# Neighbour quantiles in a four-layer graph kernel: gathers that skip pad columns, products over all partitions, and other set-up and ends

## The chip, the cores and the metric

One core of one Trainium2 chip runs the whole kernel, in one launch. The metric is device time in microseconds: the median of three runs of the kernel before is 2677.36 us. The engines are named as in the profile: PE (TensorE), PEld (PE's loading of the stationary operand), DVE (VectorE), ACT (ScalarE), POOL (GpSimd), SP (SyncE, which issues the DMAs).

## The reference

There are 32 graphs of 512 nodes with 64 channels each, in float32, and for each graph a dense 512x512 matrix of edge weights, of which about 1.6% plus the diagonal are not zero. Four layers follow one another, each as `x = layernorm(x + layer(x))`.

```python
# layer 0: A / max(deg, 1) @ x
# layer 1: Chebyshev polynomials of the normalized Laplacian, 4 orders, weights, bias
# layer 2: logmap in the hyperbolic ball for all pairs, sigmoid of an attention logit, * adj, sum
# layer 3:
adj_d = _dilate_adj(adj, mask)            # with more than 10 neighbours: each (m+1)//2-th is removed, both ways
vals = where(adj_d > 0, x[:, None], big)  # per node: the values of its neighbours (and its own), per channel
sv = sort(vals, axis=2)
m = (adj_d > 0).sum(-1)
agg = 0
for tau, wt in zip([0.25, 0.5, 0.75], [0.25, 0.5, 0.25]):
    pos = tau * (m - 1)                   # linear interpolation between the two ranks around pos
    agg += wt * (sv[floor(pos)] * (1 - frac) + sv[ceil(pos)] * frac)
h = relu((x + agg) @ W1 + b1)             # 64 -> 128
y = (h @ W2 + b2) * mask                  # 128 -> 64
...
x = layernorm(x + y)
```

The change lies around layer 3: the sort of the neighbours' values per node and channel.

## The kernel before

**Order of the work.** All 32 graphs are written out as one list of operations. A class `Order` records each operation (`seq.op`), with its engine, an estimated duration and what it reads and writes. It then orders the list by itself: each operation belongs to a lane, and each lane has a due time from a table `STAGES` (L1341, in periods of 80 us per graph, from the first operation of the lane to the last); among ready operations the earliest due goes first. For PE a penalty (`STAY`) speaks against going over to a matmul of another array shape. Every engine then gets its instructions in that fixed order. So a change in one lane moves instructions of all others. Where PE would stand idle for long, the order puts in filler matmuls (`stay_active`, L1376), which write nowhere that is read.

**Lanes.** `front` loads a graph (four 128x512 tiles of the matrix and `XA` on SP's queue), transposes the matrix on PE into `front_AT`, copied by ACT (L469), and does layers 0 and 1. `pairs` and `tail` do layer 2. The reciprocal roots of the layernorms run on POOL (L694). `graph` makes the neighbour masks, the removal, and ranks the nodes by number of neighbours: `rk` holds the position of each node in that ranking, `perm` permutes by it, `slot` numbers the neighbours of each node. `gather`, `sort` and `head` do the quantiles; `finish` and `dense` bring them back to the nodes' own order and do the small network, the last layernorm and the store.

**Strips.** With the nodes ranked by neighbour count, slot s is needed by ever fewer nodes. Nodes stand in pairs, so that 256 columns hold 512 nodes: rows 0 to 63 have the channels of one half, rows 64 to 127 those of the other. The columns are cut in two strips. `HEAD` has the first 32 columns with 24 slots and is sorted for two graphs at once, in the array `SH`; `BODY` has the rest with 11 slots, in `SB`, one graph at a time:

```python
HEAD = Strip(0, [32] * 16 + [8] * 8, 2, ...)            # first column, widths of the slots, graphs
BODY = Strip(CUT, [224] * 8 + [132, 92, 52], 1, ...)
```

A table `UP` gives for each slot how many nodes have it at most, `LO` how many at least. The widths of some slots go beyond `UP`, because the sorting network works on equal widths: those columns are pads for every graph. (An operation at the end tests the tables against the data; outside them a slower path would run.)

**gather** (L1118). For each of seven groups of columns DVE makes a one-hot matrix `gather_oh` by comparing `slot` with a constant (L449, and L445 for the small slots); PE multiplies the node values, split into three bf16 parts (`tail_x3h`), with it into a `gather_bank` in PSUM, in 24 products of 128x64 shape. Then pad products (stationary `tabs[PADS]`, moving `ohm[PADS]`, both on rows 0 to 63) add 16384 wherever a node lacks the slot's neighbour, for the columns from `LO` to the width. ACT copies the bank into `SB` and `SH`.

**sort** (L1204) runs the network of minima and maxima on DVE (L445) within `SB`. Then rank products on PE (`tabs[RANKS]` with `ohm[RANKS]`, on rows 64 to 127) give the weight of each rank for each node; DVE multiplies (`sort_prod`), PE sums by transposing into the bank `PA`, ACT copies it to `sort_ap`. The column spans of these products are rounded[...] (`spans`, L1182). **head** (L1229) does the same for two graphs, with `PRS` in place of `sort_prod`, and then calls `finish` for one graph after the other.

**finish** (L1255) transposes `rk` (128x128 float32, with `identf`) on PE to spread positions along columns, makes four masks in two steps on ACT (`head_PT`), multiplies `sort_ap` with them, adds x and calls `dense`, with its buffers `oT`, `hT`, `zo`, one of each.

**Set-up** (L505 to L668) runs once before the ordered list: constants, identity matrices, the tables `tabs` (with two DVE copies per half), the weights (small loads on SP's queue, ahead of the first graph's matrix), and memsets of `tabs`, `SB`, `SH`, `PRS` on POOL (L1368 to L1371).

Of the kernel before, what the change touches and what calls it, by code (L numbers as in the profile page):

```python
# [85 lines left out]
class Strip:  # L86
# [3 lines left out]
    def __init__(self, first, W, G, order, low):  # L90
        self.first, self.W, self.G, self.order, self.low, self.K = first, W, G, order, low, len(W)
        self.off, self.tot = {}, 0
        for s in order:
            self.off[s] = self.tot
            self.tot += W[s] * G
        self.live = [(max(lo - first, 0), min(hi - first, W[s])) for s, (lo, hi) in enumerate(needed()[:self.K])]
        self.live = [x if x[0] < x[1] else (0, 0) for x in self.live]
        self.plans = [self.plan(0), self.plan(1)]
# [71 lines left out]
    {}))  # L170
BODY = Strip(CUT, [224] * 8 + [132, 92, 52], 1, [0, 2, 1, 3, 4, 6, 5, 7, 8, 9, 10], (
    {1: (0, 1, 2, 3), 2: (0, 1), 5: (0, 1), 7: (1,), 8: (2, 3)},
    {0: (4,), 1: (1, 3), 2: (2,), 3: (0, 1, 2), 4: (0, 1), 5: (2,), 6: (1, 2), 7: (1,), 8: (3,), 9: (0, 3)}))
# [229 lines left out]
def tile_adj_resnorm(ctx: ExitStack, tc: tile.TileContext, x, adj, nodemask, w1k, b1k, att_w, att_b,  # L403
# [16 lines left out]
    pools = {}  # L420

# [79 lines left out]
    def bank(dtype=F32):  # L501
        return seq.tile(pools["ps"], [P, 512 if dtype == F32 else 1024], dtype, "bank", bufs=BANKS.get(seq.lane, 2))


# [6 lines left out]
    identh = const.tile([P, P], BF16, name="identh")  # L511
    nc.vector.tensor_copy(identh, identf)
# [12 lines left out]
    with tc.tile_pool(name="first", bufs=1) as first:  # L525
        ii = first.tile([P, N], I32, name="ii")
        nc.gpsimd.iota(ii, pattern=[[1, 2], [2, H2]], base=0, channel_multiplier=0)
        nc.vector.tensor_copy(iotap, ii)
# [21 lines left out]
    nc.vector.tensor_copy(kf, ks)  # L550
    tb = const.tile([P, K], F32, name="tb")
    ts(tb, kf, part, PAD, op0=OP.is_ge, op1=OP.mult)

    tabs = const.tile([P, K, P], F16, name="tabs")
    nc.gpsimd.memset(tabs, 0.0)
    for h in range(2):
        nc.vector.tensor_copy(tabs[h * HM:(h + 1) * HM, :, h * D:(h + 1) * D],
                              tb[h * HM:(h + 1) * HM].unsqueeze(2).to_broadcast([HM, K, D]))
    PADS, RANKS = slice(0, 2 * HM), slice(2 * HM, P)
    acc = const.tile([P, K], F32, name="acc")  # L560
    nc.vector.memset(acc, 0.0)
    tn = const.tile([P, K], F32, name="tn")
    tau = const.tile([P, 1], F32, name="tau")
    for q, w in TAUS:
        ts(tau, part, -1.0, q, op0=OP.add, op1=OP.mult)
        ts(tau, tau, 0.0, None, op0=OP.max)
        ts(tb, kf, tau, None, op0=OP.subtract)
        ts(tn, tb, -1.0, None, op0=OP.mult)
        tt(tb, tb, tn, op=OP.max)
        ts(tb, tb, -1.0, 1.0, op0=OP.mult, op1=OP.add)  # L570
        ts(tb, tb, 0.0, w, op0=OP.max, op1=OP.mult)
        tt(acc, acc, tb, op=OP.add)
    for h in range(2):
        nc.vector.tensor_copy(tabs[(h + 2) * HM:(h + 3) * HM, :, h * D:(h + 1) * D],
                              acc[(h + 2) * HM:(h + 3) * HM].unsqueeze(2).to_broadcast([HM, K, D]))
# [13 lines left out]
    nc.sync.dma_start(wk[:, :, :D], w1k.rearrange("k u c o -> (k u c) o").rearrange("(g p) o -> p g o", p=P))  # L589
    def rows(src, n, name, m):  # L590
        t = const.tile([m, n], F32, name=name)
        nc.sync.dma_start(t, bass.AP(tensor=src.tensor, offset=src.offset, ap=[[0, m], [1, n]]))
        return t

    def parts3(src, name):

        rem, n = src, src.shape[-1]
        full = const.tile([3, n], F32, name=name + "s")
        part3 = const.tile([3, n], BF16, name=name + "p")
# [12 lines left out]
    b1f = const.tile([3, D + 2], F32, name="b1f")  # L612
    nc.sync.dma_start(b1f[:, :D], bass.AP(tensor=b1k.tensor, offset=b1k.offset, ap=[[0, 3], [1, D]]))
    attb = rows(att_b, 1, "attb", P)
    bias2 = parts3(rows(b2, D, "b2f", 3), "bias2")
    meanf = const.tile([D, D], F32, name="meanf")
    nc.vector.memset(meanf, 1.0 / D)
    attw = const.tile([D, 2], F32, name="attw")
    for k in range(2):
        nc.sync.dma_start(attw[:, k:k + 1], bass.AP(tensor=att_w.tensor, offset=att_w.offset + (1 - k) * D, ap=[[1, D], [1, 1]]))  # L620
    b1c = const.tile([D, 1], F32, name="b1c")
    nc.sync.dma_start(b1c, bass.AP(tensor=b1k.tensor, offset=b1k.offset, ap=[[1, D], [1, 1]]))

    wt = const.tile([P, D], F32, name="wt")
# [8 lines left out]
    for h in range(2):  # L633
        nc.sync.dma_start(w1s[h * D:(h + 1) * D], w1)
    b1s = const.tile([HID, 1], F32, name="b1s")
    nc.sync.dma_start(b1s, b1.rearrange("(h u) -> h u", u=1))
    w2s = const.tile([HID, D], F32, name="w2s")
    nc.sync.dma_start(w2s, w2)

    nmask = const.tile([P, T, B], F32, name="nmask")  # L640
    with tc.tile_pool(name="ps_0", bufs=1, space=PSUM) as ps, tc.tile_pool(name="masks", bufs=1) as masks:
        nm8 = masks.tile([B, N], U8, name="nm8")
        nc.sync.dma_start(nm8, nodemask)
        nmf = masks.tile([B, N], F32, name="nmf")
# [10 lines left out]
        wkT = const.tile([D, P], F32, name="wkT")  # L655
# [146 lines left out]
    def order(b, res):  # L802
# [14 lines left out]
        rk = seq.tile(pools["keep"], [P, T], F32, "rk", 8)  # L817
        ts(rk, sg, -0.5, 0.5 * N - 1.0, op0=OP.mult, op1=OP.add)
        perm = seq.tile(gm, [P, T, N], F16, "perm", 1, "nbT")
# [17 lines left out]
        if b % 2 == 0:  # L837
            res["ohm"] = seq.tile(pools["keep"], [P, 2, H2], F16, "ohm", 3)
# [4 lines left out]
        act(res["ohm"][:, b % 2, :], dist, AF.Relu, bias=1.0, scale=-1.0)  # L843
        res["slots"] = slot, rk
# [273 lines left out]
    def gather(b, res):  # L1118
# [3 lines left out]
        ohm = res["ohm"]  # L1122
        sl = slot.rearrange("p j (h n) -> p j h n", h=2)
        for g in GROUPS:
            pieces, at, x = [], {}, 0
            for piece in g:
                oh = seq.tile(pools["oh"], [P, T, 2, 448], F16, "oh", 2)
                w = 0
                for k, s in piece:
                    n, c = k.W[s], k.first  # L1130
# [18 lines left out]
            for i, ((k, s), o) in enumerate(at.items()):  # L1149
                n, lo = k.W[s], max(0, LO[s] // 2 - k.first)  # L1150
                if i == len(at) - 1:
                    lo = min(lo, n - 1)
                if lo < n:
                    assert o >= pieces[-1][1]
                    mm(pt[:, o + lo:o + n], tabs[PADS, s, :], ohm[PADS, b % 2, k.first + lo:k.first + n], start=False,
                       stop=(i == len(at) - 1))

            runs = []
            for (k, s), o in at.items():
                if runs and runs[-1][0] is k and runs[-1][3] == k.off[s]:  # L1160
                    runs[-1][2] += k.W[s]
                    runs[-1][3] += k.W[s] * k.G
                else:
                    runs.append([k, o, k.W[s], k.off[s] + k.W[s] * k.G, k.off[s]])
# [18 lines left out]
    for r, (lo, hi) in enumerate(BODY.live):  # L1183
        if hi > lo:
            lo = lo - lo % 32 if lo % P > 96 else lo - lo % 64 if lo % P >= 64 else lo - lo % P
# [18 lines left out]
    def sort(b, res):  # L1204
# [6 lines left out]
        for k, rs in enumerate(RB):  # L1211
            pt = bank()
            for r, lo, hi, o in rs:
                mm(pt[:, o:o + hi - lo], tabs[RANKS, r, :], ohm[RANKS, b % 2, CUT + lo:CUT + hi], start=True, stop=True)
# [14 lines left out]
    def head(b, res):  # L1229
# [4 lines left out]
        for k, rs in enumerate(RH):  # L1234
            pt = bank()
            n = (2 * CUT, CUT)[k]
            for i, (r, _, w) in enumerate(rs):
                mm(pt[:, n * i:n * i + 2 * w].rearrange("p (c g) -> p c g", g=2), tabs[RANKS, r, :],
                   ohm[RANKS, :, :w].rearrange("p g c -> p c g"), start=True, stop=True)
# [12 lines left out]
        for g in range(2):  # L1252
            finish(b - 1 + g, res["ends"][g], ap[:, g])

    def finish(b, end, ap):  # L1255
        rk, x3 = end
        pt = bank()
        for t in range(T):
            tr(pt[:, t * P:(t + 1) * P], rk[:, t:t + 1].to_broadcast([P, P]), identf)
# [15 lines left out]
    def dense(po, x3T, x3, dst, nm):  # L1275

        fin = pools["fin"]
        oT = seq.tile(fin, [P, N], F32, "oT", 1)
# [5 lines left out]
        ph = bank()  # L1284
        mm(ph[:HID, :], w1s, oT, start=True, stop=True)
        hT = seq.tile(fin, [HID, N], F32, "hT", 1)
        act(hT, ph[:HID, :], AF.Relu, bias=b1s)
        py = bank()[:, :T * D].rearrange("p (t n) -> p t n", n=D)
# [3 lines left out]
        z = wide("zo")  # L1292
# [330 lines left out]
```

## Time and profile before

| | |
|---|---|
| median of 3 runs | 2677.36 us (2675.84 to 2685.98) |
| the profiled execution | 2680.23 us, its span 2678.4 us |
| granted TensorE clock | 0.98 |
| busy PE, DVE | 2514.1 us, 2493.2 us |
| busy ACT, POOL | 1854.6 us, 352.9 us |
| DMA | 49.96 MB, mean 19 GB/s |
| instructions | 55594 |

The span is the traced part of one execution, from its first to its last instruction. Busy times are sums over an engine's instructions; register, branch, semaphore and DMA-issuing instructions are not in them. Rows of groups read: line, engine, operation, output, inputs, partitions x elements and type, count; then busy time, mean ns of one, and the idle time just before with what ended most of it. Rows of waits read: who waits, for whom, total us, times, mean us. In a timeline a row is a start, a duration and an instruction (or several alike), with the idle time before it and what ended it in brackets.

### The profile page before, as it was taken

How to read it: one execution, taken by the hardware profiler on the slowest of the kernel's cores; microseconds unless marked ns; L12 is line 12 of the kernel's file. 1: busy time of each engine (PE TensorE's matmuls, PEld its weight loads, DVE VectorE, ACT ScalarE, POOL GpSimd, SP SyncE). 2: the span in 40 equal slices, each digit the busy share in tenths (PEclk: the TensorE clock that was granted, in tenths of full speed). 3: DMA queues.
4: the chain of work that ended last, by engine and by line, in shares of the span. 5: the costliest groups of instructions: out<-in, count | busy, mean ns of one | idle time of the engine just before them, and what ended most of it. 6: DMA issues, size and time to landing. Idle time of an engine off the chain costs nothing.

```text
span 2678.4 us, 55594 instructions
## 1 busy us (share of the span) xinstructions
PE 2514.1 (94%) x19764; PEld 1657.7 (62%) x19793; DVE 2493.2 (93%) x10191; ACT 1854.6 (69%) x4264; POOL 352.9 (13%) x329
## 2 busy tenths in 40 slices
PE   7999999999999999999999999999999999999988
PEld 5666566666666665665666666666566566666556
DVE  5689999999999999999999999999999999999993
ACT  2666768677677767777777776768767677776642
POOL 2111111111101111111111111111211111110100
PEclk9999999999999999899999999999999999999999
DMA  1100000000000000000000000000000000000000
GB/s 37 31 25 21 13 17 19 23 21 25 19 17 11 21 25 21 23 19 7 23 21 25 19 23 13 15 23 21 23 21 19 9 21 25 19 9 3 7 5 8
DMA packets 119721, 49.96 MB, mean 19 GB/s; under 512 B 53740, under 2 KB 119436, under 8 KB 119436
## 3 DMA queue, kind: packets, MB, share of 16 engines
q1 hardware_dynamic: 119436, 46.34, 6.5%
q8 instruction: 157, 2.57, 0.4%
q14 instruction: 128, 1.05, 0.1%
HBM read 37.93 MB, written 8.39 MB: 17 GB/s over the span
## 4 chain that ended last, share of the span: by engine, by line
DVE 74%; PE 18%; POOL 3%; ACT 2%; issue 2%; DMA 0%; POOLq 0%; DVEq 0%; ACTq 0%
DVE SB L445 17%; DVE SH L445 10%; DVE gather_oh L449 7%; PE front_bank L488 4%; DVE pairs_Q L445 3%; PE gather_bank L488 3%; PE pairs_bank L488 3%; DVE pairs_RW L445 3%; DVE pairs_Wt L452 2%; DVE pairs_L L452 2%; PE graph_bank L488 2%; PE head_bank L488 2%; DVE sort_prod L445 2%; DVE tail_v L445 2%; DVE pairs_EX L452 1%
## 5 line engine op out<-in xcount | busy, mean ns | idle before, releaser
L445 DVE TENSOR_TENSOR SB<-SB 128x448 f32<-128x448 f32 (+11 forms) x1424 | 573.6, 426 | 11.0
L488 PE MATMUL gather_bank<-gather_oh,tail_x3h 128*64 128x448 f16 (+2 forms) x5376 | 537.4, 332 | 4.3 <-ACT SB L469 3.7
L488 PEld LDWEIGHTS <-tail_x3h 128*64 128x64 bf16 x5376 | 303.2, 111 | 210.3 <-issue 107.9
L445 DVE TENSOR_TENSOR SH<-SH 128x128 f32<-128x128 f32 (+11 forms) x1744 | 358.3, 248 | 6.5
L488 PE MATMUL pairs_bank<-pairs_FT 67*128 67x512 f32 (+7 forms) x768 | 319.5, 519 | 19.6 <-DVE pairs_EX L452 13.8
L449 DVE TENSOR_SCALAR gather_oh<-graph_slot 128x256 f16<-128x256 f16 (+4 forms) x864 | 264.0, 352 | 10.7 <-PE gather_bank L488 10.6
L488 PE MATMUL front_bank<-front_AT,front_y 128*64 128x512 f32 x768 | 200.3, 615 | 13.0 <-DVE front_y L445 11.4
L694 POOL TENSOR_TENSOR front_rs<-front_var,mhalf 128x4 f32<-128x4 f32 x64 | 79.8, 1248 | 944.1 <-DVE front_var L449 815.8
L488 PEld LDWEIGHTS pairs_bank<-pairs_FT 67*128 67x128 f32 (+1 forms) x768 | 127.2, 195 | 78.4 <-DVE pairs_EX L452 22.2
L488 PEld LDWEIGHTS <-graph_nbT 128*128 128x128 f16 x1536 | 113.2, 99 | 82.0 <-DVE graph_do L452 23.5
L488 PE MATMUL PA<-identf,sort_prod 128*128 128x128 f32 (+4 forms) x960 | 151.0, 288 | 3.2 <-DVE sort_prod L445 2.5
L488 PE MATMUL graph_bank<-graph_perm,graph_V 128*128 128x512 f16 x512 | 135.9, 380 | 2.3 <-DVE graph_perm L449 2.0
L488 PEld LDWEIGHTS PA<-identf,sort_prod 128*128 128x128 f32 (+4 forms) x960 | 118.1, 173 | 26.7 <-issue 16.5
L488 PEld LDWEIGHTS pairs_bank<-FLS,pairs_Wt 128*128 128x128 f32 x1024 | 125.2, 192 | 14.6 <-DVE pairs_Wt L452 5.7
L469 ACT ACTIVATE graph_VP<-graph_bank 128x512 f16<-128x512 f32 x128 | 75.8, 592 | 76.8 <-PE graph_bank L488 76.2
L488 PE MATMUL pairs_bank<-FLS,pairs_Wt 128*128 128x66 f32 x1024 | 126.2, 273 | 2.0 <-DVE pairs_Wt L452 1.8
L488 PEld LDWEIGHTS front_bank<-XA,front_AT 128*128 128x128 f32 x1024 | 120.7, 192 | 9.2 <-ACT front_AT L469 3.0
L488 PE MATMUL front_bank<-XA,front_AT 128*128 128x65 f32 x1024 | 120.5, 273 | 0.8 <-ACT front_AT L469 0.6
L488 PE MATMUL head_bank<-head_PT,sort_ap 128*64 128x512 f32 x256 | 119.6, 616 | 0.6 <-ACT head_PT L469 0.6
L469 ACT ACTIVATE pairs_L<-pairs_L,pairs_oo 128x512 f32<-128x512 f32 x128 | 90.7, 719 | 40.9 <-DVE pairs_L L452 40.3
L469 ACT ACTIVATE graph_v<-graph_bank,graph_c 128x512 f16<-128x512 f32 x128 | 87.0, 680 | 43.0 <-PE graph_bank L488 22.6
L488 PE MATMUL graph_bank<-UC,graph_nbT 128*128 128x512 f16 (+3 forms) x512 | 93.7, 304 | 20.9 <-DVE graph_do L452 18.4
(327 smaller groups left out, 6169.4 us busy)
## 6 DMA issues: line engine op xcount, KB each, us to landing
front_A<-in_adj_dram SPq DMA_DIRECT2D x128, 256.0 KB, 2.8
XA<-in_x_dram SPq DMA_DIRECT2D x32, 128.0 KB, 2.2
xs<-tail_x SPq DMA_DIRECT2D x32, 128.0 KB, 2.0
out_dram<-head_zo SPq DMA_DIRECT2D x32, 128.0 KB, 2.0
wk<-in_L_gnn_weight_dram SPq DMA_DIRECT2D x1, 64.0 KB, 2.1
w1s<-in_L_gnn_W_dram SPq DMA_DIRECT2D x2, 32.0 KB, 2.2
attw<-in_L_gnn_att_W_dram SPq DMA_DIRECT2D x2, 0.2 KB, 2.3
w2s<-in_L_gnn_W_dram SPq DMA_DIRECT2D x1, 32.0 KB, 2.5
```

Source lines behind the costliest of these rows:

```text
L445: vec(lambda: nc.vector.tensor_tensor(out, a, b, op=op), out, [a, b])
L449: vec(lambda: nc.vector.tensor_scalar(out, a, s1, s2, op0=op0, **kw), out, [a], True, (s1, s2))
L452: vec(lambda: nc.vector.scalar_tensor_tensor(out, a, s, b, op0=op0, op1=op1), out, [a, b], False, (s,))
L469: 0.3, lambda: nc.scalar.activation(out, a, f, scale=scale, **kw), [out, accum_out], [a, after] + sc, table)
L488: return nc.tensor.matmul(out, w, a, start=start, stop=stop)
L694: seq.op("POOL", 0.8, 0.6, lambda: nc.gpsimd.tensor_tensor(y, v, mhalf, op=OP.pow), [y], [v])
```

## The change

1. Strips get a list of slots whose all-pad columns are not gathered (`fill`); `N` is the number of columns that are. 13, 14, 15 of `HEAD` go from 32 columns to 14, 14 and 8, 5, 6, 7 of `BODY` from 224 to 214, 196 and 168. POOL writes 16384 into the columns left out, for each graph (`BODY`) or every second (`HEAD`).
2. Pad and rank products use all 128 rows. `OHM` is a permanent array with three turns in which one half of the rows stays zero for each kind. A second ACT instruction writes the second kind. A span that begins at column 128 or above is no longer rounded down by 64 or 32 but to 128.
3. The positions kept for `finish` are a float16 copy (`rkh`), and its transposes are 16 bit.
4. Set-up: small loads go on ACT's DMA queue; `tabs`, `SB`, `SH`, `PRS` are zeroed by ACT (scale 0) in the ordered list, the tables are built there too, and two DVE copies to `tabs` per kind become ACT's. Temporaries lie in a pool `first` that is closed before the loop; the pools of the loop are opened in another order.
5. Last ends: for the last two graphs `spots` makes the position masks ahead of `head`, in buffers of `pairs`; their `finish` skips them, and the second of them has its own buffers and banks (`home`).
6. `STAGES` has other values, and a lane `ends`.

```diff
-    def __init__(self, first, W, G, order, low):
+    def __init__(self, first, W, G, order, low, fill):
+        self.N = [min(w, -(-UP[s] // 2) - first) if s in fill else w for s, w in enumerate(W)]
...
+    def bank(dtype=F32, home=None):
+        lane, seq.lane = seq.lane, home or seq.lane
...
+    def fill(a):
+        for c in range(0, a.shape[1], 768):
+            z = a[:, c:min(c + 768, a.shape[1])]
+            act(z, unit.to_broadcast(list(z.shape)), AF.Copy, scale=0.0)
...
-    nc.gpsimd.memset(tabs, 0.0)
-    for h in range(2):
-        nc.vector.tensor_copy(tabs[h * HM:(h + 1) * HM, :, h * D:(h + 1) * D],
-                              tb[h * HM:(h + 1) * HM].unsqueeze(2).to_broadcast([HM, K, D]))
+    def tables():
+        ts(tb, kf, part, PAD, op0=OP.is_ge, op1=OP.mult)
+        for h in range(2):
+            act(tabs[h * HM:(h + 1) * HM, :, h * D:(h + 1) * D],
+                                  tb[h * HM:(h + 1) * HM].unsqueeze(2).to_broadcast([HM, K, D]), AF.Copy)
...
-    nc.sync.dma_start(wk[:, :, :D], w1k.rearrange("k u c o -> (k u c) o").rearrange("(g p) o -> p g o", p=P))
+    nc.scalar.dma_start(wk[:, :, :D], w1k.rearrange("k u c o -> (k u c) o").rearrange("(g p) o -> p g o", p=P))
...
+        rkh = seq.tile(pools["keep"], [P, T], F16, "rkh", 8)
+        cp(rkh, rk)
...
-            res["ohm"] = seq.tile(pools["keep"], [P, 2, H2], F16, "ohm", 3)
+            res["ohm"] = OHM[:, b // 2 % 3]
...
-        act(res["ohm"][:, b % 2, :], dist, AF.Relu, bias=1.0, scale=-1.0)
+        for i, hm in enumerate((PADS, RANKS)):
+            act(res["ohm"][hm, i, b % 2, :], dist[hm], AF.Relu, bias=1.0, scale=-1.0)
...
+        for k, S, turn in ((BODY, SB, b % 2), (HEAD, SH, b // 2 % 2)):
+            for s in range(k.K):
+                if k.N[s] < k.W[s] and (k is BODY or b % 2 == 0):
+                    d = S[:, 2 * k.tot * turn + k.off[s] + k.G * k.N[s]:2 * k.tot * turn + k.off[s] + k.G * k.W[s]]
+                    seq.op("POOL", 0.3, 0.3, lambda d=d: nc.gpsimd.memset(d, PAD), [d], [])
...
-                    mm(pt[:, o + lo:o + n], tabs[PADS, s, :], ohm[PADS, b % 2, k.first + lo:k.first + n], start=False,
+                    mm(pt[:, o + lo:o + n], tabs[:, s, :], ohm[:, 0, b % 2, k.first + lo:k.first + n], start=False,
...
-            lo = lo - lo % 32 if lo % P > 96 else lo - lo % 64 if lo % P >= 64 else lo - lo % P
+            lo = lo - lo % 32 if 96 < lo < P else lo - lo % 64 if 64 <= lo < P else lo - lo % P
...
-                mm(pt[:, o:o + hi - lo], tabs[RANKS, r, :], ohm[RANKS, b % 2, CUT + lo:CUT + hi], start=True, stop=True)
+                mm(pt[:, o:o + hi - lo], tabs[:, r, :], ohm[:, 1, b % 2, CUT + lo:CUT + hi], start=True, stop=True)
...
-            finish(b - 1 + g, res["ends"][g], ap[:, g])
+            finish(b - 1 + g, res["ends"][g], ap[:, g], res["spots"][g] if b == B - 1 else None)
+    def spots(ends):
...
+        for g, (rk, x3) in enumerate(ends):
+            pt = bank(F16, "pairs")[:, :N]
+            for t in range(T):
+                tr(pt[:, t * P:(t + 1) * P], rk[:, t:t + 1].to_broadcast([P, P]), identb)
+            act(home[:, 2], pt, AF.Copy)
+            for i in range(4):
+                act(home[:, 3], home[:, 2], AF.Abs, bias=nposc[:, i:i + 1])
+                act(ones[g][:, i], home[:, 3], AF.Relu, bias=1.0, scale=-1.0)
+        return [(ones[0], None), (ones[1], (home, z))]
+    def finish(b, end, ap, spot):
...
+        if spot:
+            ones, home = spot
+            po = bank(home=home and "pairs")
+            for u in range(2):
+                for h in range(2):
+                    mm(po[h * D:(h + 1) * D, :], ap[:, u, h * D:(h + 1) * D], ones[:, 2 * h + u], start=(u == 0),
+                       stop=(u == 1 and h == 1), pair=True)
...
+            dense(po, None, x3, out[b:b + 1], nmask[:, :, b], home)
+            return
-            tr(pt[:, t * P:(t + 1) * P], rk[:, t:t + 1].to_broadcast([P, P]), identf)
+            tr(pt[:, t * P:(t + 1) * P], rk[:, t:t + 1].to_broadcast([P, P]), identb)
...
-    STAGES = {"front": (-0.6, 0.2), "pairs": (1.2, 1.3), "tail": (0.2, 1.5), "graph": (0.9, 1.0), "gather": (2.7, 2.9),
-              "sort": (4.5, 4.6), "head": (4.7, 5.6), "check": (3.1, 4.9)}
+    STAGES = {"front": (-0.6, -0.1), "pairs": (1.1, 1.4), "tail": (0.2, 1.5), "graph": (0.9, 1.0), "gather": (2.7, 2.9),
+              "sort": (4.5, 4.6), "head": (4.7, 5.6), "ends": (3.4, 4.8), "check": (2.4, 4.7)}
...
-        nc.gpsimd.memset(SB, 0.0)
-        nc.gpsimd.memset(SH, 0.0)
-        nc.gpsimd.memset(PRS, 0.0)
+        OHM = pools["S"].tile([P, 3, 2, 2, H2], F16, name="OHM")
+        nc.gpsimd.memset(OHM[RANKS, :, 0], 0.0)
+        nc.gpsimd.memset(OHM[PADS, :, 1], 0.0)
...
+        seq.lane, seq.batch = "gather", 0
+        fill(tabs.rearrange("p k c -> p (k c)"))
+        tables()
+        for a in (SB, SH, PRS):
+            fill(a)
...
+            if b == B - 1:
+                both["spots"] = spots(both["ends"])
```

## The prediction

> **What bounds the kernel now.** I read the busy table first, then busy time by stretch, then DVE's waits in the steady stretch, then the groups by shape, then the two ends in the timeline.
>
> ```profile
> PE 2514.1 (94%) x19764; PEld 1657.7 (62%) x19793; DVE 2493.2 (93%) x10191; ACT 1854.6 (69%) x4264; POOL 352.9 (13%) x329
> ...
> DVE 74%; PE 18%; POOL 3%; ACT 2%; issue 2%; DMA 0%; POOLq 0%; DVEq 0%; ACTq 0%
> ```
> ```profile
> 0.00:240.00 240.00, 213.87 (x1669) 150.11 (x1669) 171.75 (x637) 133.42 (x309) 36.73 (x93) 1.00 0.10 27
> 240.00:2600.00 2360.00, 2235.18 (x17588) 1459.89 (x17616) 2284.47 (x9385) 1700.25 (x3915) 312.68 (x233) 0.98 0.07 18
> 2600.00:2678.00 78.00, 65.07 (x510) 47.66 (x510) 36.97 (x172) 20.90 (x40) 3.48 (x3) 0.95 0.03 7
> ```
> In the second fence the columns after the stretch's length are PE, PEld, DVE, ACT and POOL. Two engines are nearly full, and the chain of waits says which counts: DVE. DVE's idle time is 68.3 us in the first 240 us (fill), 75.5 us in the steady 2360 us, and 41.0 us in the last 78 us. The steady idle time is little, so PE work there pays only as far as it ends DVE waits:
>
> ```profile
> DVE gather_oh L449 <- PE gather_bank L488: 8.3, 9, 2.3
> DVE front_st L686 <- PE front_bank L488: 6.1, 18, 0.6
> DVE tail_off L452 <- POOL tail_rs L694: 5.7, 8, 0.9
> DVE pairs_L L452 <- PE pairs_bank L488: 5.0, 7, 1.1
> ```
> In that answer for the steady stretch, rows that name PE add to 30.2 us, POOL 17.2, ACT 4.5. The remaining 24 us of the 75.5 are short gaps with no releaser, as between DVE instructions that need the one before.
>
> **The change, part by part. 1: gathers without pad columns.** Per graph 18, 18 and 24 columns of the head strip and 10, 28 and 56 of the body are no longer gathered, 154 of 2644.
>
> ```profile
> L488 PE MATMUL gather_bank<-gather_oh,tail_x3h 128*64 128x448 f16 x3072 | 353.5, 362 | 4.0 <-ACT SB L469 3.7
> L449 DVE TENSOR_SCALAR gather_oh<-graph_slot 128x1792 f16<-128x1792 f16 x256 | 152.2, 619 | 3.2 <-PE gather_bank L488 3.1
> L488 PE MATMUL gather_bank<-gather_oh,tail_x3h 128*64 128x256 f16 x1536 | 121.3, 281 | 0.3
> L449 DVE TENSOR_SCALAR gather_oh<-graph_slot 128x256 f16<-128x256 f16 x512 | 83.1, 220 | 2.3 <-PE gather_bank L488 2.3
> ```
> DVE: (619-220)/(1792-256) = 0.26 ns per element; 154 columns x 8 x 0.26 = 0.32 us a graph, 10.2 us in 32. PE: 353.5/3072 and 121.3/1536 give 115 and 79 ns, a slope of 0.19 ns per column; 154 x 24 products x 0.19 x 32 = 22.5 us. The pad products lose as many columns, about 2 us.
> Added for it: POOL writes 16384 into those columns, 144 memsets of 10 to 56 columns, at about 0.13 us (the 128x8 memset of XA). They stand in one queue with the reciprocal roots (1.25 us) that DVE waits for. Compared in the built program, each memset waits for a DVE instruction earlier in DVE's order than the input of the next root; so it delays a root by its own length at most. Can it stop DVE directly? Rows of the start:
>
> ```profile
> 6.99 5.69 DVE L449 TENSOR_SCALAR bias2s<-bias2p,identf 3x64 f32<-3x64 bf16 x1
> ...
> 7.37 5.26 POOL L1368 MEMSET SB<- 128x6204 f32 x1
> ```
> Three DVE instructions beside this memset end with it, though such a one takes 0.24 us elsewhere. Read from this row alone, every memset stops DVE: 144 x 0.13 = 19 us. The Trainium skill (SBUF — State Buffer, Who interferes with whom) says that a POOL instruction that only writes stops just copies and tensor-scalar instructions in a two-port mode, not those with two inputs; those are about a fifth of DVE's time here (gather_oh with 264 us and its like), which makes 4 us, or nothing where POOL is the one that waits. I take 2, and keep 0 to 19. ACT gets three more small copies and one more mask instruction a graph, about 0.9 us x 32 = 30 us at 72% load; DVE's waits for ACT were 4.5 us, so I take 0, and up to 4 if that cover fails.
>
> **2: products over all partitions.** Pad and rank products (1296) were 64*128, now 128*128, so PE changes its array shape less often. Counting changes of shape in both programs' PE order: 1252 before, 974 after. Their price:
>
> ```profile
> 1004.77 0.28 PE L493 MATMUL pairs_bank<-identf,pairs_Q 128*128 128x128 f32 x1
> 1004.98 0.74 PE L488 MATMUL gather_bank<-gather_oh,tail_x3h 128*64 128x256 f16 x10
> ...
> 1006.59 0.28 PE L493 MATMUL pairs_bank<-identf,pairs_Q 128*128 128x128 f32 x1
> 1006.70 0.38 PE L488 MATMUL graph_bank<-graph_v,identb 128*128 128x512 f16 x1
> ```
> The same transpose is followed after 0.11 us by a product of its shape, and after 0.21 us by one of another: 0.10 us a change, 28 us for 278 fewer. A rule speaks against it: the Trainium skill (TensorEngine Tiling (Array Packing), When to Use Tiling) advises half-height tiles for sums over 64 rows, for up to twice the speed. Pads (rows 0 to 63) and ranks (64 to 127) can then run side by side; if every pad product did so, 708 columns a graph x 0.42 ns (128 columns in 0.055 us) x 32 = 9.5 us of PE are lost. By the rule alone PE loses 9.5, by the row it gains 28. The trace has the two kinds mixed only in short runs, so I take 25, range -9 to 28.
> One rank product starts at column 128 in place of 192: 96 wide for 32; DVE's product with it grows from 177 to about 245 ns (92-wide rows of SB: 248), 2.2 us in 32.
>
> **3: positions in 16 bit.** 128 transposes: 0.123 us apart in f32, 0.055 in f16: PE -8.7 us. DVE gets one 128x4 copy a graph, 0.07 us in a row of independent ones, 0.20 behind its producer: 4 us.
>
> **4: order.** The scheduler's changed stages leave DVE fewer instructions directly behind the one they wait for: 716 for 808. Three dependent 128x4 rows start 0.20 us apart, independent ones 0.073: 92 x 0.12 = 11 us; more at distance two take back 3 or 4: -7.
>
> Steady sum. DVE: -10.2 + 2.2 + 4 + 2 - 7 = -9. PE loses 22.5 + 2 + 25 + 8.7 - 1 = 57 us, 1.8 us a graph, against waits whose longest is 2.5; I take half of the 30.2 us: -16 (bounds 0 and -30). Together -25.
>
> **5: set-up.** Small loads go to ACT's queue, so that SP issues the matrix at once, not at 16.97; the four POOL memsets that stopped DVE (2.2, 5.6 and 2.6 us in its row) become ACT fills.
>
> ```profile
> 16.97 1.48 SPq L497 DMA_DIRECT2D front_A<-in_adj_dram  x3
> ...
> 26.77 0.60 ACT L469 ACTIVATE front_AT<-front_bank 128x512 f32<-128x512 f32 x1 [24.74 <-DVE tb L449]
> ```
> The first transposes wait for PE's own set-up and 33 fillers (5.8 us). Without the stops the set-up ends near 15.5 in place of 20.1, so the first transposes stand near 22. Then it gives back: 18, 18 and 13 fillers between the transposes for 12 each (13 x 0.12 = 1.6 us), and fills in ACT's queue between the copies (768 columns at 0.83 ns: 0.7 us). The fourth copy comes about 1.6 us early, and two DVE table copies that stood in the path (1.9 us at 37.03) go to ACT, whose last two may hold back a copy by 1. Between 3000 PE instructions of fill stand 57 more fillers. I take -2.5; range -6 to +4.
>
> **6: last ends.** The timeline from the last PRS sum:
>
> ```profile
> 2632.44 2.00 DVE L445 TENSOR_TENSOR PRS<-PRS 128x512 f32<-128x512 f32 x5
> ...
> 2652.65 0.42 DVE L445 TENSOR_TENSOR head_zo<-head_bank,nmask 128x256 f32<-128x256 f32 x1 [18.22 <-PE head_bank L488]
> ...
> 2673.18 1.43 ACT L469 ACTIVATE head_zo<-head_zo,head_off,head_rs 128x64 f32<-128x64 f32 x4 [5.32 <-DVE head_off L452]
> ```
> 44 us after PRS two graphs are finished one behind the other, each with transposes, four masks in two steps (0.72 + 0.63) and fillers. Now the masks are made earlier on ACT (busy 3 us in 20 there), and both graphs run side by side in banks of their own. After PRS: to the copied sums 1.4, fillers 0.8, six products at 0.47 and eight of 0.26 make 4.9, copies 1.3, hidden layer and bias 4.0, DVE for both 3.9, POOL 2.5, ACT 2.0, and 3.8 to the end: 24.6. That is -19, range -15 to -22; DVE's last 24 us hold more head work in short dependent steps, which could take 2 back.
>
> Sum: -25 - 2.5 - 19 = -46.5. The profiled execution took 2680.2 us (span 2678.4), which would become 2633.7; the median of the runs is 2.9 lower, so 2631.
>
> **Rivals.** A, DVE alone is the bound: PE's relief ends no wait and the new order saves nothing; mid -2, start 0, ends -19: 2656. For it: steady DVE busy 97%. Against: 30 us of waits on PE. B, the relief ends all such waits and the order saves its 11: mid -45, start -6, ends -22: 2604. C, slower: the memsets hold POOL where roots are due, and DVE waits behind each. At 0.6 us each, 144 cost 86 beyond the sum: 2717. It decides from 46.5/144 = 0.32 us each on (slower by 0.5% from 0.42). Against: their length and their place in the order. D, the packing rule holds: PE loses only 23 us, mid -16: 2640.
>
> **How the numbers follow.** Forecast 0.66, A 0.14, B 0.11, D 0.06, C 0.03. Predicted is the likeliest, 2631. The range reaches from B's edge, 2604, to A's, 2656. 0.5% (13 us) is about what a measurement of this kernel can tell from no change. Only C lies on the other side, 0.03; A with DVE stopped for the full 19 us falls within 0.5%: 0.05.
>
> **What would show it.** DVE's steady waits on PE near 15 us for 30; gather_oh near 254 us for 264; PE busy near 2455; POOL memsets of 0.13 us with no root behind them late; first front_AT copy near 22; from the last PRS sum to the end 25 us for 44. The prediction is wrong if DVE's waits on POOL pass 30 us, if steady DVE waits on PE stay at 30, or if the second graph's end still follows the first.

## The result and the profile after

The changed kernel takes 2646.37 us (median of four runs, 2642.05 to 2650.67), the kernel before beside it 2678.47. The ratio is 0.9876, 95% interval 0.9849 to 0.9903, or 33 us less; a second comparison on another chip gave 0.9862 (0.9846 to 0.9878). The profiled execution took 2648.57 us, its span 2646.8. The forecast was 2631: the sign and the range held, and nearly a third of the forecast gain is missing. It is missing in one place, the steady stretch.

The busy table and the chain of waits of the changed kernel, from its page:

```profile
PE 2489.7 (94%) x19764; PEld 1664.5 (63%) x19790; DVE 2468.0 (93%) x10218; ACT 1893.9 (72%) x4420; POOL 351.7 (13%) x471
...
DVE 80%; PE 13%; ACT 3%; POOL 2%; issue 2%; DMA 0%; ACTq 0%; DVEq 0%; POOLq 0%
```

DVE works 25 us less. PE works 24 us less (32 in a second profile), where the prediction summed 57. Both shares stand where they stood. The stretches (fill, steady, last) show where the idle time is, in columns as before the change:

```profile
0.00:240.00 240.00, 219.66 (x1701) 156.71 (x1701) 161.91 (x643) 157.27 (x342) 30.57 (x106) 0.99 0.10 27
240.00:2570.00 2330.00, 2211.40 (x17599) 1465.14 (x17624) 2250.47 (x9330) 1717.02 (x4037) 317.01 (x361) 0.97 0.07 18
2570.00:2647.00 77.00, 58.67 (x468) 42.62 (x467) 55.60 (x248) 19.62 (x42) 4.07 (x4) 0.92 0.04 9
```

DVE's idle time is 78 us in the fill (68 before), 80 us in the steady stretch (75.5 before) and 21 us at the end (41 before). The end gained its 20 us. The fill's extra idle time is no loss by itself: DVE instructions that stood beside the four POOL memsets counted as busy before, and DVE's busy time in the fill fell by as much (161.9 us for 171.8). But the steady idle time, which was to fall by 16 us, rose by 4. DVE's waits in that stretch say on what (who waits for whom, total us, times, longest):

```profile
DVE pairs_L L455 <- PE pairs_bank L491: 13.7, 14, 1.9
DVE gather_oh L452 <- PE gather_bank L491: 11.2, 7, 3.2
DVE front_st L703 <- PE front_bank L491: 9.7, 20, 0.9
DVE tail_off L455 <- POOL tail_rs L711: 4.8, 6, 0.9
```

All rows of that answer that name PE add to 43.7 us, where 30.2 stood before and 15 were forecast; POOL's fell from 17 to 12. The row of `pairs_L` grew from 5.0 to 13.7. The groups by shape show that the work itself shrank as worked out:

```profile
L491 PE MATMUL gather_bank<-gather_oh,tail_x3h 128*64 128x448 f16 x1536 | 191.1, 361 | 0.9 <-ACT SH L472 0.9
L452 DVE TENSOR_SCALAR gather_oh<-graph_slot 128x1792 f16<-128x1792 f16 x160 | 94.5, 617 | 5.7 <-PE gather_bank L491 5.7
L491 PE MATMUL gather_bank<-gather_oh,tail_x3h 128*64 128x256 f16 x768 | 69.7, 287 | 1.7 <-ACT SH L472 1.0 <-ACT tail_x3h L472 0.7
```

Half as many products are 448 wide. Each costs 191.1/1536 = 124 ns of busy time, though, where it was 115. Four of these 9 ns come with the narrower gathers themselves (119 ns with the order kept, below). For the rest, products of other lanes now stand between them more often: counted in the traces, the gather's products run in 476 unbroken pieces, before in 416. The new memsets are cheap, 22 us of POOL for 144 (groups by line):

```profile
L1149 POOL MEMSET SB<- 128x10 f32 (+2 forms) x96 | 15.5, 164 | 652.3 <-DVE SB L448 637.9 <-ACT SB L472 14.4
L1149 POOL MEMSET SH<- 128x36 f32 (+1 forms) x48 | 6.6, 186 | 206.2 <-DVE SH L448 151.6 <-DVE PRS L448 50.5 <-ACT SH L472 4.0
```

The two ends, from the timeline (start, duration, instruction):

```profile
0.75 1.54 SPq L500 DMA_DIRECT2D front_A<-in_adj_dram  x3
...
22.00 0.60 ACT L472 ACTIVATE front_AT<-front_bank 128x512 f32<-128x512 f32 x1 [5.93 <-PE front_bank L496]
```
```profile
2621.98 2.00 DVE L448 TENSOR_TENSOR PRS<-PRS 128x512 f32<-128x512 f32 x5
...
2635.81 0.42 DVE L448 TENSOR_TENSOR head_zo<-head_bank,nmask 128x256 f32<-128x256 f32 x1 [11.84 <-PE head_bank L491]
2636.15 0.41 DVE L448 TENSOR_TENSOR tail_ends<-pairs_bank,nmask 128x256 f32<-128x256 f32 x1
```

The matrix is issued at 0.75 us and the first copy of `front_AT` stands at 22.00, as forecast. From the last PRS sum (2623.98) to the end it is 22.8 us, where it was 44.0: the second graph, `tail_ends`, follows 0.34 us behind the first. So the last ends and the first copy came out as forecast. The last PRS sum, however, comes only 10.5 us earlier, where the steady stretch alone was to bring 25.

### The profile page after: what moved, and what is told of

Its sections match the earlier page's. It is cut to its first block, busy times and chain, and to the rows that moved or that the text cites. A ratio compares the mean times of both kernels' runs of the same rounds, so it can differ in the third digit from the quotient of the medians.

```text
span 2646.8 us, 55900 instructions
## 1 busy us (share of the span) xinstructions
PE 2489.7 (94%) x19764; PEld 1664.5 (63%) x19790; DVE 2468.0 (93%) x10218; ACT 1893.9 (72%) x4420; POOL 351.7 (13%) x471
## 4 chain that ended last, share of the span: by engine, by line
DVE 80%; PE 13%; ACT 3%; POOL 2%; issue 2%; DMA 0%; ACTq 0%; DVEq 0%; POOLq 0%
DVE SB L448 18%; DVE SH L448 10%; DVE gather_oh L452 7%; DVE pairs_Q L448 4%; DVE pairs_RW L448 3%; PE pairs_bank L491 3%; PE front_bank L491 3%; DVE pairs_Wt L455 3%; PE graph_bank L491 2%; PE gather_bank L491 2%; DVE sort_prod L448 2%; DVE pairs_L L455 2%; DVE tail_v L448 2%; DVE pairs_RW L455 2%; DVE pairs_EX L448 2%
## 5 line engine op out<-in xcount | busy, mean ns | idle before, releaser
L491 PE MATMUL gather_bank<-gather_oh,tail_x3h 128*64 128x448 f16 (+5 forms) x5376 | 528.7, 323 | 5.8 <-ACT SB L472 2.9
L452 DVE TENSOR_SCALAR gather_oh<-graph_slot 128x256 f16<-128x256 f16 (+9 forms) x864 | 250.4, 338 | 13.4 <-PE gather_bank L491 13.4
L491 PE MATMUL front_bank<-front_AT,front_y 128*64 128x512 f32 x768 | 188.5, 603 | 20.7 <-DVE front_y L448 18.1
L491 PEld LDWEIGHTS pairs_bank<-pairs_FT 67*128 67x128 f32 (+1 forms) x768 | 134.1, 198 | 89.3 <-issue 27.7
L491 PE MATMUL PA<-identf,sort_prod 128*128 128x128 f32 (+3 forms) x960 | 142.8, 282 | 2.4 <-DVE sort_prod L448 2.3
L491 PEld LDWEIGHTS front_bank<-XA,front_AT 128*128 128x128 f32 x1024 | 126.0, 196 | 11.8 <-ACT front_AT L472 3.0
L491 PEld LDWEIGHTS PA<-identf,sort_prod 128*128 128x128 f32 (+3 forms) x960 | 121.3, 176 | 12.3 <-issue 6.6
L491 PEld LDWEIGHTS <-tabs 128*128 128x128 f16 x1296 | 80.5, 100 | 68.5 <-issue 54.5
L472 ACT ACTIVATE graph_V<-graph_bank 128x512 f16<-128x512 f32 x128 | 75.6, 591 | 66.8 <-PE graph_bank L491 66.3
L491 PEld LDWEIGHTS front_bank<-front_AT,front_y 128*64 128x64 f32 x768 | 50.8, 136 | 96.7 <-issue 62.5
L491 PE MATMUL head_bank<-head_PT,sort_ap 128*64 128x512 f32 x240 | 110.3, 613 | 0.1
```

The lines of the kernel that those rows point to most:

```text
L452: vec(lambda: nc.vector.tensor_scalar(out, a, s1, s2, op0=op0, **kw), out, [a], True, (s1, s2))
L472: 0.3, lambda: nc.scalar.activation(out, a, f, scale=scale, **kw), [out, accum_out], [a, after] + sc, table)
L491: return nc.tensor.matmul(out, w, a, start=start, stop=stop)
```

## The experiments

Each row of the table is a comparison with the kernel before, run beside it on one chip. Differences below are differences of these ratios, times 2680 us; the intervals of two ratios make about 5 to 8 us of uncertainty for such a difference.

| kernel | ratio (95%) |
|---|---|
| before, full rows, order kept | 0.9995 (0.9988 to 1.0001) |
| before, narrow gathers, order kept | 0.9940 (0.9927 to 0.9954) |
| before, new due times of front and pairs | 1.0116 (1.0095 to 1.0137) |
| changed | 0.9862 (0.9846 to 0.9878) |
| changed, no early masks | 0.9924 (0.9910 to 0.9938) |
| changed, old set-up | 0.9872 (0.9853 to 0.9892) |
| changed, old due times of pairs | 0.9841 (0.9826 to 0.9855) |
| changed, old due times of front | 0.9807 (0.9793 to 0.9821) |
| changed, old due times of front, pairs, check | 0.9787 (0.9773 to 0.9800) |
| changed, front due at 0.35 | 0.9852 (0.9831 to 0.9874) |
| old front times, half rows | 0.9912 (0.9894 to 0.9930) |
| old front times, float32 positions | 0.9831 (0.9812 to 0.9850) |

**Full rows in the old order.** Any edit of a duration or a shape makes the planner order everything anew, so two experiments record the old operation and issue the new one.

```diff
-    def mm(out, w, a, start, stop, pair=False, opens=None):
+    def mm(out, w, a, start, stop, pair=False, opens=None, run=None):
...
-            return nc.tensor.matmul(out, w, a, start=start, stop=stop)
+            return nc.tensor.matmul(out, *(run or (w, a)), start=start, stop=stop)
...
-                       stop=(i == len(at) - 1))
+                       stop=(i == len(at) - 1), run=(tabs[:, s, :], ohm[:, b % 2, k.first + lo:k.first + n]))
```

> The kernel before with its instruction order kept to the last instruction; only the 1296 pad and rank products run over 128 rows in place of 64 (one table for both kinds, so pad sums also hold rank weights and the other way round; nothing else differs). 330 changes of PE's shape between half and full rows vanish. Theory A (the prediction: such a change costs 0.10 us): PE busy falls by about 33 us, to 2481, and the time by 9 to 17 us. Theory B (a change between half and full rows costs nothing; only runs of products with 64 columns lose time when they are cut): PE busy within 5 us of before, the time within 4 us. The rule on half-height tiles: PE busy up by up to 9.5 us, the time up by up to 5.

The time fell by 1.3 us (ratio 0.9995). The busy table:

```profile
PE 2499.5 (93%) x19793; PEld 1669.4 (62%) x19793; DVE 2493.2 (93%) x10191; ACT 1854.1 (69%) x4264; POOL 355.8 (13%) x329
```

PE's busy time fell by 14.6 us; 29 products of `PA` are without a record in the profile of before (19764 matmuls for 19793), at 0.40 us each in this one, so the fall is up to 26 us, or 0.04 to 0.08 us for each of the 330 changes that vanished. PE behaves like theory A at a somewhat lower price, the time like theory B. PE's freed time ended hardly any wait: DVE's steady waits on PE add to 28.9 us, for 30.2 before. By the rule of the Trainium skill that spoke against full rows (TensorEngine Tiling (Array Packing), When to Use Tiling) PE would have lost up to 9.5 us, by the prediction's estimate; in this kernel's short scattered products its time fell.

**Narrow gathers in the old order.** The same device in `gather`, with the widths `k.N` issued where `k.W` is recorded.

```diff
-                        ts(oh[:, :, :, w:w + n], sl[:, :, :, c:c + n], 2.0 * s + 1.0, None, op0=OP.is_equal)
+                        ts(oh[:, :, :, w:w + n], sl[:, :, :, c:c + n], 2.0 * s + 1.0, None, op0=OP.is_equal,
+                           run=(oh[:, :, :, v:v + m0], sl[:, :, :, c:c + m0]))
...
+                               run=(pt[h * D:(h + 1) * D, o1:o1 + v], x3h[:, q, j, :], oh[:, j, h, :v]))
```

> The kernel before with its instruction order kept; only the gathers are narrower by the 154 pad columns a graph (one-hot, products, pad products, copies). The columns left out are not written at all and the copies are packed, so some slots land in wrong columns; no other work is left out. By the rows of before, DVE busy falls by 10 and PE busy by 22 to 25 us. If both reliefs reach the end (the prediction's sum) the time falls by 15 to 22 us; if DVE alone is the bound, by 10; if PE alone, by 22; if the fixed order gives the saving back as waits elsewhere, by under 5.

16 us less, and DVE's busy time 10.0 us less. The busy table, and the widest gather products:

```profile
PE 2494.9 (94%) x19793; PEld 1651.0 (62%) x19793; DVE 2483.2 (93%) x10191; ACT 1851.6 (69%) x4264; POOL 348.6 (13%) x329
```
```profile
L489 PE MATMUL gather_bank<-gather_oh,tail_x3h 128*64 128x448 f16 x1536 | 182.5, 365 | 2.1 <-ACT SB L470 2.1
```

PE lost 19.2 (up to 31 with the missing records). The products with `gather_oh` together kept PE busy for 514.5 us, before for 537.4: 22.9 less, as forecast (22.5). DVE's steady waits on PE fell from 30.2 to 24.3 us. The gain is thus the sum of DVE's 10 us and of 6 us of waits: of PE's 19 to 31 us about a quarter was paid here, and of the full rows' 15 to 26 us less than a tenth.

**Without the early masks.**

```diff
-            if b == B - 1:
-                both["spots"] = spots(both["ends"])
...
-            finish(b - 1 + g, res["ends"][g], ap[:, g], res["spots"][g] if b == B - 1 else None)
+            finish(b - 1 + g, res["ends"][g], ap[:, g], None)
```

> The changed kernel without the early masks and the parallel end: the last two graphs are finished like all others, one behind the other. From the last sum of PRS to the end the traces have 44.0 us before and 22.8 after. If the ends gain all of that, this kernel is 21 us slower than the changed one, about 2667 us. If the early masks take back some of it in the stretch before (ACT and PE of the last two graphs), it is only 12 to 16 us slower.

16.6 us slower than the changed kernel (0.9924 for 0.9862; 13 by the first comparison, 0.9876). The timeline has the last PRS sum and the second graph's product:

```profile
2617.02 2.00 DVE L448 TENSOR_TENSOR PRS<-PRS 128x512 f32<-128x512 f32 x5
...
2654.19 0.42 DVE L448 TENSOR_TENSOR head_zo<-head_bank,nmask 128x256 f32<-128x256 f32 x1 [13.84 <-PE head_bank L491]
```

From 2619.0 to its end at 2662.7 it is 43.7 us, 20.9 more than in the changed kernel. The 4 us of difference lie ahead of the sum, which comes 1.4 to 5 us earlier here than in the two profiles of the changed kernel.

**Old due times.** First front, pairs and check together:

```diff
-    STAGES = {"front": (-0.6, -0.1), "pairs": (1.1, 1.4), ...
+    STAGES = {"front": (-0.6, 0.2), "pairs": (1.2, 1.3), ...
```

> The changed kernel with the old due times of front, pairs and check. The prediction's step 4 had the new due times save 7 us on DVE: then this kernel takes about 2653 us. Rival: the new due times cut the gathers' runs of 64-column products into more pieces (436 pieces of 5376 products with the new ones, 399 with the old ones, counted in the recorded order), at about 0.3 us of PE a cut: then PE busy is about 10 us lower here and the time is equal or up to 6 us less than the changed kernel's.

Both expectations fell short: this kernel is not slower, nor 6 us faster, but 20 to 24 us faster than the changed one (0.9787 for 0.9862 and 0.9876). PE's busy time is 13.7 us less (up to 24 with the changed kernel's 26 missing records), as the rival had it or more, but that is not all. The new due times, which I had put down as a gain of 7 us, cost three times that. To tell the lanes apart, together with the changed kernel again:

> The changed kernel once more, unaltered, so that the kernels of this comparison stand beside it on the same chip. If the first measurement holds, its ratio to the kernel before is 0.985 to 0.990; the early masks would then be worth the difference to the kernel without them, 0.9924.

> The changed kernel with the old due times of front alone (its last operations due 0.3 periods later). Theory F (the earlier end of front is what costs 24 us: its short dependent steps, with their roots on POOL, are put ahead of work that would have covered them): about 24 us faster than the changed kernel, DVE's steady waits on POOL near 4 us in place of 12. Theory P (the wider window of pairs costs it): within 6 us of the changed kernel, and DVE's waits for pairs_bank stay near 17 us. If it is the luck of one order, anything between, without a trend in these waits.

> The changed kernel with the old due times of pairs alone. Theory P: about 24 us faster than the changed kernel, DVE's steady waits for pairs_bank fall from 17 to near 5 us. Theory F: within 6 us of the changed kernel, and the waits on POOL stay near 12 us.

Front alone brings 15 us (2626.8 for 2643.0 us on the same chip), pairs alone 5.6 with intervals that overlap; the two add up to what all three brought. Neither theory holds as it was put: front brings less than F's 24 us, and pairs' waits fall with front's times too. DVE's waits in the steady stretch of the changed kernel, second profile:

```profile
DVE pairs_L L455 <- PE pairs_bank L491: 13.8, 14, 1.5
DVE front_st L703 <- PE front_bank L491: 10.3, 21, 0.9
DVE gather_oh L452 <- PE gather_bank L491: 9.9, 8, 2.4
DVE tail_off L455 <- POOL tail_rs L711: 4.8, 6, 0.9
```

and with front's old due times:

```profile
DVE gather_oh L452 <- PE gather_bank L491: 8.2, 12, 2.0
DVE front_st L703 <- PE front_bank L491: 7.1, 18, 0.8
DVE pairs_L L455 <- PE pairs_bank L491: 2.6, 3, 1.5
...
DVE tail_off L455 <- POOL tail_rs L711: 1.1, 2, 0.9
```

All waits of the stretch from 240 to 2540 us add to 54.7 us in the first and 30.0 in the second: on PE 40.0 for 23.2, on POOL 11.8 for 3.6. The waits fall by 24.7 us, the spans of the two profiles differ by 18.3: the whole difference in time is there, and it lies in the waits of three lanes (front, pairs, tail), not of front alone. With pairs' old times alone the row of `pairs_L` falls as far, to 2.9 us, but all waits only to 49.0.

What did PE do while DVE waited for it? For 32 of the 40 us it worked on the very lane that DVE waited for, and for 16 of the 23 with front's old times; on other lanes it worked for 8 and 7 us (worked out from both engines' timelines, each moment given to the product that began last). So the added waits are not time that PE gave to another lane: DVE's instruction stands in its order too soon after the products that it needs. Whether PE began these products late because other lanes held it before, is not shown.

**A later end still.**

```diff
-    STAGES = {"front": (-0.6, -0.1),
+    STAGES = {"front": (-0.6, 0.35),
```

> The changed kernel with front's end due still later, at 0.35 in place of 0.2 (old) and -0.1 (changed). From -0.1 to 0.2 the time fell by 16 us. If the waits keep falling with front's later end: 3 to 8 us below the one with 0.2. If 0.2 is near the best point: within 5 us of it; if front's later end now delays pairs and all behind it: over 5 us slower.

12 us slower than at 0.2. The waits are low (33.5 us in all, for 30.0), though those on POOL are back at 9.3, and DVE's busy time is 3.5 us more; this explains some 7 of the 10 us between the two profiles, and the rest stays open. There is no trend to follow: of the three values tried the old one is best, and a shift of 0.15 periods moves the time by 12 us.

**The due times alone.**

```diff
-    STAGES = {"front": (-0.6, 0.2), "pairs": (1.2, 1.3),
+    STAGES = {"front": (-0.6, -0.1), "pairs": (1.1, 1.4),
```

> The kernel before with the new due times of front and pairs and nothing else. If these due times cost what they cost in the changed kernel, it is 15 to 22 us slower than before, DVE's steady waits on PE and POOL above 60 us for 47. If the new due times fit the old kernel and only jar with the shorter gathers: within 6 us of before. The prediction's step 4 would have it 7 us faster.

31 us slower, more than any of the three expectations. The profiled execution was the fastest of its four and 20 us slower than that of before. Its waits:

```profile
DVE gather_oh L449 <- PE gather_bank L488: 16.2, 15, 2.4
DVE pairs_L L452 <- PE pairs_bank L488: 15.3, 17, 2.0
DVE front_st L686 <- PE front_bank L488: 13.2, 28, 1.1
```

The rows of `pairs_L` and `front_st` have grown as in the changed kernel, to 15.3 and 13.2 us from 5.0 and 6.1. All rows add to 73.0 us for 51.6, about these 20 us. So the due times cost time without the other parts of the change as well.

**Full rows in a new order.** On the kernel with front's old times, pad and rank products go back to 64 rows, known to the planner.

```diff
-                    mm(pt[:, o + lo:o + n], tabs[:, s, :], ohm[:, 0, b % 2, k.first + lo:k.first + n], start=False,
+                    mm(pt[:, o + lo:o + n], tabs[PADS, s, :], ohm[PADS, 0, b % 2, k.first + lo:k.first + n], start=False,
...
-                mm(pt[:, o:o + hi - lo], tabs[:, r, :], ohm[:, 1, b % 2, CUT + lo:CUT + hi], start=True, stop=True)
+                mm(pt[:, o:o + hi - lo], tabs[RANKS, r, :], ohm[RANKS, 1, b % 2, CUT + lo:CUT + hi], start=True, stop=True)
```

> The changed kernel with the old due times of front (0.9807 of the kernel before), but with pad and rank products on 64 rows again. In a kept order the full rows were worth nothing (0.9995). Theory S (a third array shape binds the order: the penalty for a change of shape holds products back): this kernel is 6 to 15 us slower than the one with full rows, DVE's steady waits on PE over 30 us in place of 23. Rival: the rows cost nothing in any order: within 4 us.

28 us slower (0.9912 for 0.9807), twice the upper end of theory S. PE's busy time is 38 us more than with full rows (28 if 25 missing records of that profile are counted at 0.40 us). The rows:

```profile
PE 2514.1 (95%) x19837; PEld 1660.6 (62%) x19837; DVE 2474.8 (93%) x10218; ACT 1883.4 (71%) x4410; POOL 337.4 (13%) x471
```
```profile
DVE gather_oh L452 <- PE gather_bank L491: 23.1, 17, 2.9
```

`gather_oh` waits 23.1 us for PE, 8.2 with full rows: a gather's bank and its one-hot buffers come free later. All waits add to 56.6 us for 30.0. In a kept order PE's relief was worth 1 us, so most of the 28 us comes with the new order. Theory S puts that down to one shape less, but only one pair of orders was compared: how much of the 28 us is this and how much the luck of one order stays open; the 12 us between two due times above are a measure of such luck.

**Positions and set-up.**

> The changed kernel with the old due times of front, but with the positions kept and transposed in float32 again. The prediction's terms: PE 8.7 us more, DVE 4 to 5 us less (no copy). If DVE alone counts, it is 4 us faster than the one with 16 bit (0.9807 of the kernel before); if PE's time counts in full, up to 5 us slower; the sum of both is within 3 us.

```diff
-        rkh = seq.tile(pools["keep"], [P, T], F16, "rkh", 8)
-        cp(rkh, rk)
...
-            tr(pt[:, t * P:(t + 1) * P], rk[:, t:t + 1].to_broadcast([P, P]), identb)
+            tr(pt[:, t * P:(t + 1) * P], rk[:, t:t + 1].to_broadcast([P, P]), identf)
```

6 us slower, intervals that overlap (0.9831 for 0.9807). This shows no more than that the 16-bit positions cost nothing that could be seen.

> The changed kernel with the old set-up's order of things: SB, SH, PRS and tabs are zeroed by POOL memsets before the ordered list, the tables are built before it, and the small loads go on SP's queue ahead of the first matrix. The prediction gave the new set-up 2.5 us (range -6 to +4 for its cost): this kernel is then 2.5 us slower than the changed one, and its first front_AT copy stands near 27 us in place of 22. If the fills in ACT's queue and the fillers had taken all back, the times are equal; if the whole shift of the first copy is kept, it is 5 us slower.

```diff
-    nc.scalar.dma_start(wk[:, :, :D], ...
+    nc.sync.dma_start(wk[:, :, :D], ...
...
-        fill(tabs.rearrange("p k c -> p (k c)"))
-        tables()
-        for a in (SB, SH, PRS):
-            fill(a)
+        for a in (SB, SH, PRS):
+            nc.gpsimd.memset(a, 0.0)
```

0.9872 for 0.9862: 2.7 us by the ratios, with intervals that overlap, so it cannot be told from nothing. The first copy of `front_AT` stands at 27.37 us and the fourth at 35.76, for 21.80 and 29.30 in the changed kernel; at most half of these 6 us reach the end. The old set-up itself was not that late: in the kernel before, the fourth copy stood at 32.01 us, so the change brought it forward by 2.5 to 2.7 us. This experiment shifts more than the change did and does not measure the change's own gain.

## Why the prediction was right or wrong

- Part 1, gathers: right in a kept order. DVE 10.0 us for 10.2, PE 19 to 31 for 24.5, and 16 us of time. Memsets of 0.15 us for 0.13 hold up no root, since DVE's waits on POOL fell: rival C is out. Nor do they stop DVE. In the changed kernel's trace 217 DVE instructions from 40 us on ran beside one of them, and all together they took 0.3 us more than the usual time of their kind; the prediction allowed 2 us, at most 19.
- Part 2, full rows: the price of a change of shape was near (0.04 to 0.08 us for 0.10), though it was read from one pair of rows with a change of columns, not of rows. The step from PE's time to the end was wrong: in a kept order 15 to 26 us of PE gave 1.3 us (interval 0 to 3).
- Part 3: the transposes' busy time fell from 20.6 to 12.9 us (7.7 for 8.7), DVE's copies took 2.6 us for 4; in the time it is too small to be told.
- Part 4, order: the wrong step. I counted DVE instructions directly behind the DVE instruction they wait for, found 92 fewer and called it -7. For DVE's own time that is not refuted: beside the terms that can be named (`gather_oh` -10.2, `sort_prod` +2.0, the copies +2.6) its busy time after the first 40 us fell by another 9 us, worked out from its timeline. With the old due times of front, pairs and check it fell by 7 of these too, so the due times bring little of it. The count sees no wait on another engine, and those are what the due times changed: +15 us for front, and about +5 for pairs; +31 on the kernel before.
- The steady sum: DVE's own part was right in kind (its busy time fell by 25 us, of which 11 belong to the set-up, so 14 for 9 forecast). "I take half of the 30.2 us" had no ground, and its bounds, 0 and -30, did not let the waits grow: in the changed kernel the waits on PE rose to 40 to 44, which the prediction named as a sign that it is wrong. With front's old times they fell to 23.2.
- PE's relief in that sum was too large as well, 24 to 32 us for 57. The gather products give 22.9 us with the order kept, but in the changed kernel they still take 528.7 us of PE, 8.7 less than before. The new order took the rest back, and the sum has no term for this.
- Part 5: the first copy at 22.0 as forecast, the fourth 2.5 us earlier for 1.6; the fills took 0.82 us each for 0.7. The time, 2.5 forecast, was not measured by itself.
- Part 6: right in kind, 21.2 us after the last PRS sum for 19, of which some 13 to 17 reach the total.
- A sum among the rivals: B's own terms give -43 for the steady stretch, or the -45 written there only if the memsets' 2 us are left out as well.

So the time fell between forecast and rival A, a little nearer to A, and not for A's reason: PE's relief can end waits (6 us with the gathers alone), but the new due times made more than that. That the time stayed inside the range is in part luck: the range allowed for a relief without effect, not for a term of the wrong sign. With front's old due times the same change takes 0.9807 or, with those of pairs and check too, 0.9787 of the time before, 52 to 57 us less, which is more than was forecast. These two kernels (2626.8 and 2626.7 us, medians on different chips) are the fastest here.

## What to carry to other kernels

Where a planner fixes the order, cost an edit twice: once with the order kept (record the old operation, issue the new one), once with the order made anew; here the same full rows were worth 1 us in the first and up to 28 in the second. Relief of an engine that is not the bound pays only as far as it ends the bound's waits: about a quarter of it in one of the two cases measured, under a tenth in the other. So list those waits and see which would end before taking a share. And change due times by themselves and last: here they cost a third of what the change could gain, while the gathers and the last ends did what they were made for.

## What I had not expected

The planner's due times weigh about as much as the largest parts of the change (16 us for the gathers, 13 to 17 for the last ends): a shift of front's last due time by 0.3 periods is 15 us, by 0.15 beyond that 12 us in the other direction, without an instruction added or removed but for fillers. The granted clock is no guide to this: the kernel with front due at 0.35 ran at 0.981 to 0.987 and took 12 us more, by the ratios, than the one with 0.2, which ran at 0.975 to 0.979.
